# Rearranging the last steps before the scans of a state-space layer: B by TensorE, a square root by ScalarE, another order of loads and matmuls

## The chip, the cores and the metric

The kernel runs on one core of a Trainium2 chip. A core has five engines with their own instruction streams: TensorE (PE) for matmuls and transposes, VectorE (DVE), ScalarE (ACT), GpSimd (POOL), and SyncE (SP), which here only issues DMAs. They meet through semaphores. SBUF is the working memory of 128 partitions, PSUM the memory that matmuls write, DRAM the large memory outside, reached by DMA. The metric is device time in microseconds (us); several runs are made and their median is compared.

## The reference

Four layers follow one another, each normalised, applied and added to the residual x of 2 x 512 tokens by 512: a Mamba layer, a feed-forward layer with 4-bit weights, an attention over heads within each token, and a latent mixture layer. The change lies in the first layer; it also touches when the 4-bit weights of the second are unpacked. Cut to that:

```python
proj = hidden_states @ W_in.T                  # 512 -> 2 x 1024
x, gate = proj[..., :D_IN], proj[..., D_IN:]
x = silu(causal depthwise convolution of x with K = 4 taps, plus conv_b)
ssm = x @ W_x.T                                # 1024 -> 32 + 16 + 16
ts, Bm, Cm = ssm[..., :R], ssm[..., R:R + N], ssm[..., R + N:]
ts, Bm, Cm = rms_forward(ts), rms_forward(Bm), rms_forward(Cm)
dt = softplus(ts @ W_dt.T + b_dt)
A = -exp(A_log)
def step(state, inp):                          # state: 1024 channels x 16
    dt_t, B_t, C_t, u_t = inp
    state = state * exp(dt_t[..., None] * A) + (dt_t * u_t)[..., None] * B_t[:, None, :]
    return state, einsum('bdn,bn->bd', state, C_t)
y = (scan of step over 512 tokens + x * D) * silu(gate)
out = y @ W_out.T
```

`rms_forward` divides by the root of the mean square plus 1e-6, for ts, B and C apart. The weights of the second layer are `q * s - (z + 1) * s` with 4-bit q, eight to a 32-bit word.

## The kernel before

Channels lie on partitions, in 8 chunks of 128, and the 512 tokens of a batch in the free dimension. The two batches are b = 0 and 1. Code up to line 643 is the head; lines 650 to 1115 are the scan stage.

**The head** normalises x of batch 0 and transposes it (lines 570 to 585), then loops over the chunks c (line 593): TensorE projects a chunk into PSUM (`px`, line 597), ScalarE evicts it with one tap and the bias (`evict_x`, 468), VectorE adds three taps (`conv`, 475), ScalarE applies Silu (609), and TensorE multiplies the chunk by W_x into the 64 rows of ts, B and C for each token (`ranks_of`, 489). TensorE is two chunks ahead of the ranks.

**Words.** Beside that loop the 4-bit weights are unpacked. A "word" here is one of the eight 4-bit places of the packed gate and up weights for one cut of 512 columns; the head does two cuts, so 16 words (`GateUpWords`, lines 235 to 307). For each, VectorE extracts the nibble (233) and subtracts the zero points (293), GpSimd multiplies by the scales (295) and issues a DMA of 256 KB to DRAM (300). Three words are begun before the first convolution and finished after it; each later chunk has one or two (lines 605 to 616), and three stand around the norm of the ranks (618 to 634). A word's result lies in one of four rotating buffers, which is free once its DMA has landed.

**The last chain.** When the last chunk's ranks are there, the gate of chunk 0 is projected (626, four float32 matmuls, which the trace shows as eight passes). `ranks_norm` (494) squares on ScalarE, reduces on VectorE, raises to the power -0.5 on GpSimd (508) and multiplies on VectorE. TensorE transposes the result (524) to rows (`pt`). `ranks_out` (527) copies B and C rows to SBUF (`bc`), sends them to DRAM (`scr`, 531) and copies ts to `dtT`. `states` (535) then reads each group of two B or C rows back from `scr`, broadcast to 128 partitions: 16 loads of 512 KB on SP's queue, B0, C0, B1, C1 and so on. Behind them on SP's queue stand the four tiles of x of batch 1 (`load_x`, 641), then weights. dt of chunk 0 is a matmul (548) and a Softplus (553).

**The scan stage.** For each batch and chunk there are 8 scans s of two states each. ScalarE makes exp(dt A) into one of two PSUM tiles `da` (1002); VectorE multiplies `du` = dt u by B into `bx` (`times_B`, 1018) and scans (`scan`, 1022); GpSimd multiplies by C (`times_C`, 1028); TensorE sums over states with an identity matrix (1050). `du` lies in PSUM. The order on each engine is the order of the loop at line 1072, which `pin` (401) fixes; other work (gates, the projection of batch 1, its norm `norm_job`, the last eight words) is run in turns by `tick` (671). In that order `bn_stats` on the first tile of batch 1's x stands on VectorE between scans 4 and 5, and `times_B(2)` in front of scan 1. At most 8 DMAs of SP's queue are under way: an issue waits until the eighth before it has landed.

Of the kernel before, what the change touches and what calls it, by code (L numbers as in the profile page):

```python
# [9 lines left out]
F32 = mybir.dt.float32  # L10
F16 = mybir.dt.float16
I32 = mybir.dt.int32
AF = mybir.ActivationFunctionType
# [43 lines left out]
def tile_sandwich(  # L57
# [177 lines left out]
    class GateUpWords:  # L235
# [9 lines left out]
            word_loads(self.parts(zds), n0, n1, qw, z, s, 2, eng, engz)  # L245
            return [(n0, n1, qw, z, s, q, w, j) for j in range(PACK)]

        def start(self, dq, zds):
            def tl(dt, tag, bufs):
                return lambda name: dq.tile([P, CW], dt, tag=tag, name=f"{tag}_{name}", bufs=bufs)  # L250

            self.todo = []
            for a in range(2):
                nm = f"gu{a}"
                self.todo += self.cut(
                    a,
                    (tl(I32, "qw", 2)(nm), tl(F16, "z", 2)(nm), tl(F16, "s", 2)(nm),
                     tl(I32, "q", 3), tl(F32, "w", 4)),
                    zds, nc.gpsimd, nc.sync,
                )  # L260

# [9 lines left out]
                zds, nc.sync, nc.sync,  # L271
            )

        def steps(self):
            n0, n1, qw, z, s, q_, w_, j = self.todo.pop(0)
            n, nm = n1 - n0, f"gu{n0}_{j}"
            q = q_(nm)
            beside = bool(scans)

            while beside and (now[0] % 2 == 0 or pool_at[0] == (now[0] - 1) // 2 - 1):  # L280
                yield 1
            nibble(q[:, :n], qw[:, :n], j)
            yield 2
            w = w_(nm)
            if beside:
                nc.scalar.copy(w[:, :n], q[:, :n])
                yield 2
                yield from pool_turn()
                nc.gpsimd.tensor_sub(w[:, :n], w[:, :n], z[:, :n])
                yield 1  # L290
                yield from pool_turn()
            else:
                nc.vector.tensor_sub(w[:, :n], q[:, :n], z[:, :n])
                yield 2
            nc.gpsimd.tensor_mul(w[:, :n], w[:, :n], s[:, :n])
# [9 lines left out]
        def word(self):  # L305
            for _ in self.steps():
                pass

    def once(dq):
# [112 lines left out]
    with ExitStack() as mamba:  # L422
# [30 lines left out]
            dtT.append(t_)  # L453
        wx = smp.tile([P, NCH, N_ROW], F32, name="wx")
        nc.gpsimd.dma_start(out=wx, in_=W_x)
        Bbs = [[None] * NGI for _ in range(B)]
        Cbs = [[None] * NGI for _ in range(B)]
        st = {}
# [35 lines left out]
        def ranks_norm(b, ps):  # L494

            sq = jrow(f"sq{b}")[:, : TB * N_ROW].rearrange("p (i r n) -> p i r n", i=TB, n=N_ST)
            nc.scalar.activation(sq.rearrange("p i r n -> p i (r n)"), ps, AF.Square)
            yield 2
            ss = stat.tile([P, TB, 3], F32, tag="ss", name=f"ss{b}")
            nc.vector.tensor_reduce(  # L500
                ss[:, :, 0], sq[:, :, : R_DT // N_ST].rearrange("p i r n -> p i (r n)"), AX.X, ALU.add
            )
            nc.vector.tensor_reduce(ss[:, :, 1:], sq[:, :, R_DT // N_ST :], AX.X, ALU.add)
            r = stat.tile([P, TB, 3], F32, tag="rr", name=f"rr{b}")
            nc.vector.tensor_scalar(r[:, :, 0], ss[:, :, 0], 1.0 / R_DT, 1e-6, ALU.mult, ALU.add)
            nc.vector.tensor_scalar(r[:, :, 1:], ss[:, :, 1:], 1.0 / N_ST, 1e-6, ALU.mult, ALU.add)
            yield 1
            nc.gpsimd.tensor_tensor(r, r, mhalf3, ALU.pow)
# [16 lines left out]
            return pt  # L525

        def ranks_out(b, pt):
            bc = jrow(f"bc{b}")
            nc.vector.tensor_copy(bc[R_B:N_ROW], pt[R_B:N_ROW])
            sc = dram.tile([N_ROW - R_B, S], F32, tag=f"scr{b}", name=f"scr{b}")  # L530
            nc.sync.dma_start(out=sc, in_=bc[R_B:N_ROW])
            scr.append(sc)
            nc.scalar.copy(dtT[b][:R_DT, :], pt[:R_DT])

        def states(b, gi):

            for lst, lo, nm in ((Bbs[b], 0, "B"), (Cbs[b], R_C - R_B, "C")):
                t_ = bcp.tile([P, NG, S], F32, tag=f"{nm}{gi}", name=f"{nm}{b}_{gi}")
# [7 lines left out]
        def dt_in(b, c):  # L546
            ps = mbank(f"pv{b}_{c}")
            nc.tensor.matmul(ps, wdt[:, ts(c, P)], dtT[b], start=True, stop=True)
            return ps

# [8 lines left out]
        with ExitStack() as p1:  # L559
# [28 lines left out]
            gw.start(dq, zds)  # L588
            nc.vector.tensor_scalar(A, A, -1.0, None, ALU.mult)
            diag(0)  # L590

# [1 line left out]
            for c in range(NCH):  # L593
                w = w_in(0, 0, c)
                ps = bank1(c, f"px0_{c}")
                for k in range(KH):
                    nc.tensor.matmul(
                        ps, w[:, k, ts(c % 2, P)], xT[0][:, k, :], start=(k == 0), stop=(k == KH - 1)
                    )
                    if k == 1 and c >= 2:  # L600
                        for i in range(TB):
                            ranks_of(0, c - 2, i, pr)
                uc = u[0][c] = new_u(f"u0_{c}")
                evict_x(c, ps, uc)
                early = [gw.steps() for _ in range(3 if c == 0 else 0)]
                for word in early:
                    next(word)
                conv(c, ps, uc)
                nc.scalar.activation(uc, uc, AF.Silu)
                for word in early:  # L610
                    for _ in word:
                        pass
                if c:
                    gw.word()
                if c in (2, 4, 6):
                    gw.word()

            late = gw.steps()
            for _ in range(2):
                next(late)  # L620
            for c in (NCH - 2, NCH - 1):
                for i in range(TB):
                    ranks_of(0, c, i, pr)
            pg = mbank("pg0_0")
            for k in range(KH):
                nc.tensor.matmul(
                    pg, w_in(1, 0, 0)[:, k, 0:P], xT[0][:, k, :], start=(k == 0), stop=(k == KH - 1)
                )
# [12 lines left out]
            with tc.issue_after(last.ins):  # L641
                load_x(1)
            pin()
# [6 lines left out]
        with ExitStack() as p2:  # L650
# [7 lines left out]
            das = []  # L658
            for i, ps_da in enumerate((ps_da0, ps_da1)):
                da = ps_da.tile([P, NG, S], F32, tag=f"da{i}", name=f"da{i}")  # L660
                nc.vector.memset(da[:, :, 0:1], 0.0)
                das.append(da)


            jobs = []
# [38 lines left out]
            MM = 0.86  # L704
            STEP = 3.5

            def in_proj(b, ps, w, e):
                for k in range(KH):
# [10 lines left out]
            def gate(b, c):  # L719
                w = w_in(1, b, c)  # L720
                if c + 2 - c % 2 < NCH:
                    w_in(1, b, c + 2 - c % 2)
                ps = yield from bank(f"pg{b}_{c}")
                yield from in_proj(b, ps, w, c % 2)
                spawn(gate_job(b, c, ps), 2)

            def x_job(c, ps):
# [709 lines left out]
```

## Time and profile before

| what | us |
|---|---|
| runs: median (lowest to highest) | 954.11 (953.85 to 956.48) |
| the profiled execution, its own time | 955.89 |
| its span, first to last instruction | 954.1 |
| VectorE busy from 24 to 50 us, in the convolution loop | 24.53 of 26.00 |
| TensorE's granted clock, 50 to 56 and 56 to 64 us | 0.71, 0.58 |
| TensorE idle in front of the last ranks, waiting for Silu | 4.1 |
| VectorE, start of the first and the last convolution | 20.00, 52.88 |
| VectorE, start of scans 0, 1 and 2 | 73.97, 80.03, 83.34 |
| VectorE idle in front of `times_B(0)` and `times_B(2)`, for B | 3.74, 1.32 |
| VectorE busy from 110 to 200 us, in the scan stage | 89.38 of 90.00 |

A row of the timeline gives the start, the length, the engine, the line, the instruction with what it writes and reads, how many, and in brackets how long the engine was idle before it and what ended that. "PEld" is the load of a matmul's weights, "SPq" an issue on SP's queue. Rows of one kind that follow each other are merged.

### The profile page before, as it was taken

To read this page: it belongs to the slowest core of one execution; us is meant where nothing else is said; L and a number is where in the kernel's file an instruction comes from. 1 tells how busy PE (TensorE), PEld (TensorE's weight loads), DVE (VectorE), ACT (ScalarE), POOL (GpSimd) and SP (SyncE) were. 2 spreads that over 40 slices of the span, in tenths; PEclk is the share of its full clock that TensorE was granted. 3 is DMA by queue.
4 is the path that set the end of the run, shared out by engine and by line. 5 is a ranking of instruction groups with operands and counts; after the bars stand their busy time and mean duration, and the time that the engine had idled before them with its cause. 6 is when DMAs were issued, how large, how long until landed. Compare 5 with 4: busy or idle time off the path is not lost.

```text
span 954.1 us, 7148 instructions
## 1 busy us (share of the span) xinstructions
PE 862.3 (90%) x2184; PEld 386.6 (41%) x2184; DVE 675.2 (71%) x783; ACT 420.2 (44%) x631; POOL 484.0 (51%) x351
## 2 busy tenths in 40 slices
PE   6977989779989899579999999998999998999994
PEld 3532434333534434234433444444544444445441
DVE  4968999999999998999999995535610034534225
ACT  3335775656666655476655640125320014322122
POOL 5665796777877777876877884440000000011002
PEclk9978999898999989889999999999999999998997
DMA  6439211010002854300111103455223221200101
GB/s 182 163 124 387 69 37 38 30 37 31 22 23 83 297 187 152 89 0 0 45 44 45 30 9 124 150 159 198 58 64 89 58 89 45 66 12 30 48 0 44
DMA packets 43816, 80.08 MB, mean 84 GB/s; under 512 B 7774, under 2 KB 20937, under 8 KB 43778
## 3 DMA queue, kind: packets, MB, share of 16 engines
q1 hardware_dynamic: 41506, 73.64, 23.6%
q0 software_dynamic: 1984, 5.47, 1.6%
q10 hardware_dynamic: 288, 0.52, 0.2%
q8 instruction: 17, 0.28, 0.1%
q14 instruction: 21, 0.17, 0.1%
HBM read 68.37 MB, written 11.24 MB: 83 GB/s over the span
## 4 chain that ended last, share of the span: by engine, by line
PE 46%; DVE 28%; issue 11%; POOL 5%; DMA 2%; ACT 1%; SPq 0%; DVEq 0%; POOLq 0%; ACTq 0%
DVE bx L1022 11%; DVE bx L1018 8%; PE pd L1365 6%; PE py L1050 5%; PE pup L1302 5%; PE fo L1155 4%; PE fu L367 3%; PE fo L1218 3%; POOL bx L1028 3%; PE fg L367 3%; PE fu L947 3%; PE fg L947 3%; PE po L1133 3%; PE po L916 2%; DVE u L475 2%
## 5 line engine op out<-in xcount | busy, mean ns | idle before, releaser
L1028 POOL TENSOR_TENSOR bx<-bx,C 128x1024 f32<-128x1024 f32 x128 | 302.0, 2360 | 115.3 <-DVE bx L1022 90.7
L1022 DVE TENSOR_TENSOR_SCAN bx<-da,bx 128x1024 f32<-128x1024 f32 x128 | 291.6, 2279 | 0.1
L1050 PE MATMUL py<-bx,ident 128*128 128x512 f32 x480 | 238.1, 626 | 35.6 <-POOL bx L1028 32.3
L1002 ACT ACTIVATE da<-dt,A 128x511 f32<-128x511 f32 x256 | 176.3, 691 | 161.6 <-DVE bx L1022 155.7
L1018 DVE TENSOR_TENSOR bx<-du,B 128x1024 f32<-128x1024 f32 x128 | 154.4, 1206 | 9.0 <-DMA B<-scr 5.1
L1050 PEld LDWEIGHTS py<-bx,ident 128*128 128x128 f32 x480 | 91.5, 198 | 164.1 <-issue 93.1
L1231 DVE TENSOR_TENSOR it<-it,fu 128x512 f32<-128x512 f32 (+1 forms) x11 | 7.6, 688 | 72.3 <-PE fu L367 72.3
L1302 PE MATMUL pup<-hT_l,wup 128*128 128x512 f32 x128 | 57.5, 604 | 0.0
L381 POOL TENSOR_TENSOR sd<-ve,half 128x4 f16<-128x4 f16 x2 | 2.1, 1045 | 109.0 <-DVE ve L379 109.0
L709 PE MATMUL pg<-xT,w_g 128*128 128x512 f32 x120 | 57.1, 604 | 0.0
L1365 PE MATMUL pd<-wdn,hid 128*128 128x512 f32 x128 | 55.3, 592 | 0.0
L127 POOL TENSOR_TENSOR rs_lo<-ve_lo,mhalf 128x1 f32<-128x1 f32 x8 | 5.5, 684 | 78.0 <-DVE ve_lo L125 78.0
L947 PE MATMUL fg<-hT_f,wg 128*128 128x512 f32 (+1 forms) x88 | 42.1, 597 | 0.0
L475 DVE SCALAR_TENSOR_TENSOR u<-px,ch,u 128x511 f32<-128x511 f32 (+2 forms) x48 | 35.8, 746 | 7.0 <-ACT u L468 5.9
L367 PE MATMUL fg<-hT_f,wg 128*128 128x512 f32 (+1 forms) x88 | 40.2, 593 | 0.7 <-ACT hT_f L171 0.7
L947 PE MATMUL fu<-hT_f,wu 128*128 128x512 f32 (+1 forms) x88 | 40.7, 592 | 0.0
L367 PE MATMUL fu<-hT_f,wu 128*128 128x512 f32 (+1 forms) x88 | 39.8, 593 | 0.0
L1218 PE MATMUL fo<-wd,it 128*128 128x512 f32 (+1 forms) x88 | 39.6, 592 | 0.0
L1155 PE MATMUL fo<-wd,it 128*128 128x512 f32 (+1 forms) x88 | 38.0, 593 | 1.6 <-DMA wd<-wd_d 1.6
L1365 PEld LDWEIGHTS pd<-wdn,hid 128*128 128x128 f32 x128 | 24.2, 190 | 30.7 <-issue 30.1
L1302 PEld LDWEIGHTS pup<-hT_l,wup 128*128 128x128 f32 x128 | 24.5, 195 | 28.8 <-issue 28.8
L1230 ACT ACTIVATE it<-fg 128x512 f32<-128x512 f32 (+1 forms) x11 | 6.6, 597 | 65.7 <-PE fg L367 65.7
(224 smaller groups left out, 1161.4 us busy)
## 6 DMA issues: line engine op xcount, KB each, us to landing
wo<-in_W_outT SPq DMA_DIRECT2D x20, 512.0 KB
B<-scr SPq DMA_DIRECT2D x16, 512.0 KB
C<-scr SPq DMA_DIRECT2D x16, 512.0 KB
wg<-wgu_d SPq DMA_DIRECT2D x10, 512.0 KB
wu<-wgu_d SPq DMA_DIRECT2D x10, 512.0 KB
w_x<-in_W_in SPq DMA_DIRECT2D x8, 512.0 KB
wgu_d<-w_gu POOLq DMA_DIRECT2D x16, 256.0 KB, 2.3
w_g<-in_W_in SPq DMA_DIRECT2D x8, 512.0 KB
```

Of the source, the lines that this page charges most:

```text
L367: nc.tensor.matmul(ps[:m], w[:, kc, e * P : e * P + m], hT[:, kc, :], start=(kc == 0), stop=(kc == KH - 1),)
L709: nc.tensor.matmul(ps, w[:, k, ts(e, P)], xT[b][:, k, :], start=(k == 0), stop=(k == KH - 1))
L947: nc.tensor.matmul(ps[:m], wt[j][a][:, kc, e * P : e * P + m], hT[:, kc, :], start=(kc == 0), stop=(kc == KH - 1),)
L1002: nc.scalar.activation(das[s % 2][:, i, 1:], st["dt", b, c][:, 1:], AF.Exp, scale=A[:, c, n : n + 1])
L1018: nc.vector.tensor_mul(bx, st["du"].unsqueeze(1).to_broadcast([P, NG, S]), Bbs[b][gi])
L1022: nc.vector.tensor_tensor_scan(flat, das[s % 2].rearrange("p n t -> p (n t)"), flat, 0.0, ALU.mult, ALU.add)
L1028: nc.gpsimd.tensor_mul(bxs[s], bxs[s], Cbs[b][s % NGI])
L1050: nc.tensor.matmul(st["y"], ident, bx[:, i, :], start=False, stop=last)
L1155: nc.tensor.matmul(fo[t], its[i][:m, ts(t, P)], w[:m, e], start=(i == 0), stop=(i == len(IC) - 1),)
L1218: nc.tensor.matmul(fo[t], its[i][:m, ts(t, P)], w[:m], start=(i == 0), stop=(i == len(IC) - 1),)
L1302: nc.tensor.matmul(ps, w[:, kc, ts(e, P)], src[kc], start=(kc == 0), stop=(kc == KH - 1))
L1365: nc.tensor.matmul(pd, hid[kc][:, ts(i, P)], wdn[kc], start=(kc == 0), stop=(kc == INT // P - 1),)
```

## The change

- The norm of batch 0's ranks takes a square root on ScalarE and a reciprocal on VectorE in place of the power on GpSimd. A root of one column stands on ScalarE between the gate's Silu and the norm; the function table for the root is loaded there.
- B's first group comes to the first product from TensorE, which multiplies the rows `bc` by `pick`, a matrix of copied identity columns that GpSimd makes at the start, into the second `da` tile. The first product reads dt u from SBUF (`d0`) and B from there; the copy of dt u to PSUM comes after it.
- Loads from `scr` go in the order B1, C0, B2, C1, ..., B7, C6, C7, B0. x stays behind them.
- The gate of chunk 0 is projected in front of the last chunk's ranks; half of the gate of chunk 1 stands in front of the transposes, its other half in the scan stage. `pt` and the first dt use other PSUM banks. ts is copied out of `pt` before B and C.
- Of the 16 words, four are begun before the first convolution, and two of these subtracted before it. Words 6, 7, 10 and 13 (counted from 0) are converted by ScalarE and subtracted by GpSimd. The last word stands behind the copy of B and C. Nibbles have four buffers, and the last four words' results lie in buffers of the gates.

As the program is built, VectorE's statistics of x still stand between scans 4 and 5, and `times_B(2)` in front of scan 1; VectorE's copy of B and C waits for ScalarE's copy of ts, since both read the same tile. On ScalarE a word's conversion stands between Silu of a chunk and the next chunk's eviction.

```diff
@@ words
-        def start(self, dq, zds):
+        def start(self, dq, zds, apart):
...
-                     tl(I32, "q", 3), tl(F32, "w", 4)),
+                     tl(I32, "q", 4), lambda n: apart(n) or tl(F32, "w", 4)(n)),
...
-        def steps(self):
+        def steps(self, eng=nc.vector):
...
             w = w_(nm)
-            if beside:
+            if eng is nc.vector:
+                eng.tensor_sub(w[:, :n], q[:, :n], z[:, :n])
+                yield 2
+            else:
                 nc.scalar.copy(w[:, :n], q[:, :n])
                 yield 2
-                yield from pool_turn()
-                nc.gpsimd.tensor_sub(w[:, :n], w[:, :n], z[:, :n])
+                if beside:
+                    yield from pool_turn()
+                eng.tensor_sub(w[:, :n], w[:, :n], z[:, :n])
...
@@ head
+        pick = trow("pick")[:, : NG * P].rearrange("p (n q) -> p n q", n=NG)
+        for n in range(NG):
+            nc.gpsimd.tensor_copy(pick[:, n, :], ident[:, R_B + n : R_B + n + 1].to_broadcast([P, P]))
...
-            nc.gpsimd.tensor_tensor(r, r, mhalf3, ALU.pow)
+            if b:
+                nc.gpsimd.tensor_tensor(r, r, mhalf3, ALU.pow)
+            else:
+                nc.scalar.activation(r, r, AF.Sqrt)
+                nc.vector.reciprocal(r, r)
...
         def ranks_out(b, pt):
-            bc = jrow(f"bc{b}")
+            bc = st["bc"] = jrow(f"bc{b}")
+            nc.scalar.copy(dtT[b][:R_DT, :], pt[:R_DT])
             nc.vector.tensor_copy(bc[R_B:N_ROW], pt[R_B:N_ROW])
...
-            nc.scalar.copy(dtT[b][:R_DT, :], pt[:R_DT])
...
-                early = [gw.steps() for _ in range(3 if c == 0 else 0)]
+                early = [gw.steps() for _ in range(4 if c == 0 else 0)]
                 for word in early:
                     next(word)
+                for word in early[:2]:
+                    next(word)
                 conv(c, ps, uc)
...
-                if c in (2, 4, 6):
-                    gw.word()
-            late = gw.steps()
-            for _ in range(2):
-                next(late)
-            for c in (NCH - 2, NCH - 1):
-                for i in range(TB):
-                    ranks_of(0, c, i, pr)
+                for _ in range((0, 0, 2, 0, 1, 0, 1, 0)[c]):
+                    gw.word(nc.gpsimd)
+            for i in range(TB):
+                ranks_of(0, NCH - 2, i, pr)
             pg = mbank("pg0_0")
...
-            for n, _ in enumerate(ranks_norm(0, pr)):
-                if n == 2:
-                    for _ in late:
-                        pass
-                    gw.word()
-                    gw.word()
+            for i in range(TB):
+                ranks_of(0, NCH - 1, i, pr)
             g[0][0] = new_g0("g0_0")
             nc.scalar.activation(g[0][0], pg, AF.Silu)
-            ranks_out(0, ranks_rows(0, mbank("pt0")))
+            root = stat.tile([P, 1], F32, tag="root", name="root", bufs=1)
+            nc.scalar.activation(root, half[:, 0:1], AF.Sqrt)
+            half_gate = mbank("pg0_1")
+            for k in range(KH // 2):
+                nc.tensor.matmul(
+                    half_gate, w_in(1, 0, 0)[:, k, P : 2 * P], xT[0][:, k, :], start=(k == 0), stop=False
+                )
+            for _ in ranks_norm(0, pr):
+                pass
+            ranks_out(0, ranks_rows(0, bank1(0, "pt0")))
             for gi in range(NGI):
-                last = states(0, gi)
-            dt_out(0, 0, dt_in(0, 0))
+                if gi + 1 < NGI:
+                    states(0, gi + 1, "B")
+                states(0, gi, "C")
+            last = states(0, 0, "B")
+            gw.word()
+            dt_out(0, 0, dt_in(0, 0, bank1(0, "pv0_0")))
@@ scan stage
+            B0 = das[1]
+            for n in range(NG):
+                nc.tensor.matmul(
+                    B0[:, n, :], pick[R_B : R_B + N_ST, n, :], st["bc"][R_B : R_B + N_ST],
+                    start=True, stop=True,
+                )
+            nc.vector.memset(das[0][:, :, 0:1], 0.0)
...
-            new_du(0)
+            d0 = jrow("d0")
+            nc.vector.tensor_mul(d0, u[0][0], st["dt", 0, 0])
+            st["du"] = ps_du.tile([P, S], F32, tag="du", name="du0_0")
             exps(0)
+            bxs[0] = bxp.tile([P, NG, S], F32, tag="bx", name="bx0_0_0")
+            nc.vector.tensor_mul(bxs[0], d0.unsqueeze(1).to_broadcast([P, NG, S]), B0)
+            nc.scalar.copy(st["du"], d0)
+            nc.vector.memset(das[1][:, :, 0:1], 0.0)
             exps(1)
-            times_B(0)
```

More of the change, by code (lines that the diff above doesn't have):

```diff
@@ L278, in steps @@
             beside = bool(scans)
+            if beside:
+                eng = nc.gpsimd
             while beside and (now[0] % 2 == 0 or pool_at[0] == (now[0] - 1) // 2 - 1):
@@ L284, in steps @@
             w = w_(nm)
-            if beside:
+            if eng is nc.vector:
+                eng.tensor_sub(w[:, :n], q[:, :n], z[:, :n])
+                yield 2
+            else:
                 nc.scalar.copy(w[:, :n], q[:, :n])
                 yield 2
-                yield from pool_turn()
-                nc.gpsimd.tensor_sub(w[:, :n], w[:, :n], z[:, :n])
+                if beside:
+                    yield from pool_turn()
+                eng.tensor_sub(w[:, :n], w[:, :n], z[:, :n])
                 yield 1
[L291 to L294, printed above, removed]
+                if beside:
+                    yield from pool_turn()
             nc.gpsimd.tensor_mul(w[:, :n], w[:, :n], s[:, :n])
@@ L303, in steps, with word @@
             yield 2
-        def word(self):
-            for _ in self.steps():
+        def word(self, eng=nc.vector):
+            for _ in self.steps(eng):
                 pass
@@ L532, in ranks_out, with states @@
             scr.append(sc)
-            nc.scalar.copy(dtT[b][:R_DT, :], pt[:R_DT])
-        def states(b, gi):
+        def states(b, gi, which="BC"):
             for lst, lo, nm in ((Bbs[b], 0, "B"), (Cbs[b], R_C - R_B, "C")):
+                if nm not in which:
+                    continue
                 t_ = bcp.tile([P, NG, S], F32, tag=f"{nm}{gi}", name=f"{nm}{b}_{gi}")
@@ L544, in states, with dt_in @@
             return ins
-        def dt_in(b, c):
-            ps = mbank(f"pv{b}_{c}")
+        def dt_in(b, c, ps=None):
+            ps = ps or mbank(f"pv{b}_{c}")
             nc.tensor.matmul(ps, wdt[:, ts(c, P)], dtT[b], start=True, stop=True)
@@ L587, in tile_sandwich @@
             zds = zeros(dz, [gate_z, up_z], KH, INTER, "gu")
-            gw.start(dq, zds)
+            apart = [f"gu{CUTS[1][0] * PW}_{j}" for j in range(PACK - 4, PACK)]
+            gw.start(dq, zds, lambda n: new_g0(f"w_{n}") if n in apart else None)
             nc.vector.tensor_scalar(A, A, -1.0, None, ALU.mult)
@@ L660, in tile_sandwich @@
                 da = ps_da.tile([P, NG, S], F32, tag=f"da{i}", name=f"da{i}")
-                nc.vector.memset(da[:, :, 0:1], 0.0)
                 das.append(da)
+            B0 = das[1]
[5 more added lines that the diff above has]
+            nc.vector.memset(das[0][:, :, 0:1], 0.0)
             jobs = []
@@ L705, in tile_sandwich, with in_proj @@
             STEP = 3.5
-            def in_proj(b, ps, w, e):
-                for k in range(KH):
+            def in_proj(b, ps, w, e, k0=0):
+                for k in range(k0, KH):
                     nc.tensor.matmul(
@@ L722, in gate @@
                     w_in(1, b, c + 2 - c % 2)
-                ps = yield from bank(f"pg{b}_{c}")
-                yield from in_proj(b, ps, w, c % 2)
+                if (b, c) == (0, 1):
+                    turns.append([f"pg{b}_{c}", None])
+                    ps = half_gate
+                    yield from in_proj(b, ps, w, c % 2, KH // 2)
+                else:
+                    ps = yield from bank(f"pg{b}_{c}")
+                    yield from in_proj(b, ps, w, c % 2)
                 spawn(gate_job(b, c, ps), 2)
```

## The prediction

> **What bounds the kernel now.** I read the chain of waits first, then the timeline from the convolution loop to the sixth scan, then the DMA share by window. The chain of waits, up to 100 us (start, length, what):
>
> ```profile
> 51.48 1.47 DVE w_gu L293
> ...
> 57.93 5.95 PE pg L626 x8
> ...
> 65.07 2.49 DMA scr<-bc
> ...
> 69.52 9.34 DMA B<-scr
> ...
> 93.36 0.61 DVE st_n L761
> ```
>
> Up to 56 us VectorE's convolutions and its work on the 4-bit words set the pace. Then eight gate passes of 0.74 us hold the transposes, the round trip of B and C through DRAM follows, and from 80 us VectorE is dense: nearly all that follows to 330 us is its products and scans. A shift of the scans' start should therefore reach the end, unless a later VectorE instruction waits for something that did not shift. The timeline (start, length, engine, line, instruction) shows the three places that decide:
>
> ```profile
> 27.26 1.76 DVE L233 TENSOR_SCALAR q_gu<-qw_gu 128x512 int32<-128x512 int32 x1
> ...
> 27.55 1.17 POOL L295 TENSOR_TENSOR w_gu<-w_gu,s_gu 128x512 f32<-128x512 f32 x1
> ...
> 33.17 1.27 POOL L295 TENSOR_TENSOR w_gu<-w_gu,s_gu 128x512 f32<-128x512 f32 x1 [1.31 <-DVE w_gu L293]
> ...
> 33.52 1.47 DVE L293 TENSOR_TENSOR w_gu<-q_gu,z_gu 128x512 f32<-128x512 int32 x1
> ...
> 59.16 2.40 POOL L508 TENSOR_TENSOR rr<-rr,mhalf 128x12 f32<-128x12 f32 x1 [0.56 <-DVE rr L506]
> ...
> 83.88 4.01 SPq L83 DMA_DIRECT2D x<-in_x_in  x4
> ...
> 93.28 0.68 DVE L761 BATCH_NORM_STATS2 st_n<-x 128x6 f32<-128x512 f32 x1
> ...
> 95.27 0.34 SPq L111 DMA_DIRECT2D w_x<-in_W_in  x1
> ```
>
> First: a nibble or subtraction of VectorE that meets a GpSimd multiply lasts until that ends (1.76 for 0.42, 1.47 for 0.69). Second: the power on GpSimd takes 2.40 us. Third: the statistics of batch 1's x stand between scans 4 and 5 on VectorE. The last row waited 0.33 us for the fourth x, so the four x (256 KB, 0.62 us apart at the stream's rate) land near 93.2, 93.9, 94.5 and 95.2. The first is just in time for 93.28. By windows the 16 DMA engines are full from 76 to 91 us (share 1.02 and 1.03, 420 GB/s): B, C and x are one stream, each half megabyte 1.24 us behind the last (issues at 76.33, 77.58, 78.88 wait each for a landing).
>
> **The change, part by part.** Times count from E, the end of the last convolution (55.19 before).
>
> *The loop.* A step from one convolution to the next took 3.73 us with one word, 5.25 with two. Now three steps carry GpSimd words: VectorE saves the subtraction, but ScalarE converts the nibble (0.47 for 352 columns at L286, 0.57 for a 512 copy at L1010; I take 0.6) ahead of the next eviction, and GpSimd subtracts too (0.85 for 352 columns at L289, so 1.2 for 512).
> - Convolution 1 to 2: two subtractions now run before convolution 0, in VectorE's idle 5.1 us, so GpSimd starts its queue some 5 us sooner and the nibble of 27.26 finds it free: 4.64 becomes 3.8, -0.85.
> - 2 to 3: 2.31 of convolution, 0.42 + 0.69 + 0.5 for a word and a nibble, the next nibble held 1.2 by the multiply, 0.6 + 0.7 for conversion and eviction: 6.4 for 5.25, +1.15, with three words instead of two.
> - 3 to 4: GpSimd has 2 x 3.3 us of words 6 and 7 (1.2 + 1.17 + 0.9 of DMA issue); a hold of 0 to 0.65, +0.1 taken.
> - 4 to 5: a nibble held 1.1 by word 8's multiply, then subtraction, nibble, conversion: 6.2 for 5.25, +0.95.
> - 5 to 6: a nibble held: +0.25. 6 to 7: 0.
>
> Sum +1.6. Bounds: with no hold at all, -0.4 (0.85 gained, 0.4 for the third word in the second step); with a hold of 0.36 us on average (60% of GpSimd's time in such work, 0.6 us left of one) for each of the 14 nibbles and subtractions behind convolution 2, +5.0 - 0.85 = +4.2. I take the sum, the hits being placed one by one.
>
> [...]
>
> *Square root on ScalarE.* Silu (0.63), the gate's Silu (0.54 apart, 0.60 long), a table load of 1.28 and a 128x1 root (0.2) end at E+2.7; the Square ends at E+3.1, as before (58.35, E+3.16). The last ranks are ready at E+1.9, since the gate's eight passes (0.43 each, as at 50 us) now fill TensorE's 4.1 us of idle in front of them: the table load takes that gain. Reductions and scaling: 0.72, E+3.85. Root 0.2 and reciprocal 0.23 (178 ns for 128x4 at L383, 550 for 128x64 at L1268) with two hand-overs, E+4.45, then 0.5 of products: E+4.97 against E+6.89.
>
> [...] Here the load at 65.67 lasts 1.28 and the next ACTIVATE starts at 66.96, 0.01 behind it. [...]
>
> *Transposes.* The half gate's four passes end at E+3.7, before the rows are ready. Transposes E+5.05 to E+5.65, against E+9.13. The copy of dt's rows now goes first (0.57), and B and C (0.68) wait for it: E+7.05, and scr is sent at E+7.08 against E+9.88: -2.8. If TensorE's clock is halved (passes of 0.86, as after the 4.1 us idle), the half gate ends at E+6.3 and 1.3 to 1.8 of it is lost.
>
> *B by TensorE.* B0 needs two matmuls of 16 rows, four passes, at most 2.2 us; dt is ready at E+8.2, d0 at E+8.9 to E+10.1 (word 15's multiply may hold it), the product at E+11 at most, the exponentials (1.28 + 1.41) at E+10.9, scan 0 ends near E+13.4, 70.2 us against 76.26. Only scan 1 waits for that, and it waits for B2 longer: cover of over 4 us. The two copies that make `pick` cost nothing: 4.44 + 2 x 0.40 (a 128x128 product on GpSimd) ends before 5.29, when the first power comes; at worst 0.1.
>
> *Order of B and C.* B2, for which scan 1 waits (78.86), goes from fifth to third in SP's queue: 2 x 1.24 = 2.5 us sooner. C0 stays second (75.1 before, by the issue that waited for it) and comes with the shift of scr alone, 73.9, behind scan 0 and well ahead of scan 1's turn at GpSimd. B0 goes last, and is needed only for chunk 1. Scan 1 then starts 1.2 + 2.5 = 3.7 sooner.
>
> *What is late next.* x still stands seventeenth. VectorE reaches its statistics at 93.28 - 3.7 = 89.6, and x lands at 93.2 - 1.2 = 92.0. It waits 2.4 us, and scan 5 with everything queued behind it (products, scans, so GpSimd's C products and TensorE's sums) moves by the shift of scr alone.
>
> **Sum:** +1.6 - 2.8 = -1.2 us; the order's 2.5 us are given back at x. Span 954.1 - 1.2 = 952.9. The profiled run took 955.89, 1.8 more than its span; the median of the runs, 954.11, is close to the span, so the shift is put on it: **952.9 us**.
>
> **The rivals.**
> 1. *The loop costs nothing* (-0.4): 2.8 + 0.4 = 3.2, 950.9. For it: VectorE has three fewer subtractions there. Against: each converted word sits on ScalarE between Silu and eviction, where the step's length is set.
> 2. *x does not bind*, the stream is faster or the statistics can wait: 3.7, 950.4. Against: full DMA engines and x arriving on time to 0.1 us.
> 3. *The port takes it all* (slower): holds of +4.2 in the loop, net +1.4: 955.5. Place: nibbles at L233 beside GpSimd's subtract and multiply pairs. It decides from a loop loss of 2.8 us. For it: 2.23 us for one 352-column nibble at 142.32. Against: between these pairs GpSimd issues its DMA for 0.9 us.
> 4. *The transposes still wait* (TensorE at half clock): -1.2 + 1.8 = +0.6, 954.7. Against: idles of 0.86 and 1.96 us left passes at 0.43; the longest idle now would be 1.8.
>
> **How the numbers follow.** Forecast 0.50 (own range 951.5 to 954.2), rivals 0.15, 0.10, 0.15, 0.10. The range 949.9 to 956.0 takes in the rivals' middles and a scatter like that of the three runs. A measurement of this kernel can tell 0.3%, 2.9 us, from no change: below 951.2 lie most of rivals 1 and 2 and a tail of the forecast, 0.24; above 957.0 only a tail of rival 3, 0.08; between them 0.68.
>
> **What would show it.** Right: the last convolution starts near 54.5 (52.88 before), scr is issued near 63.9, scan 1 starts near 76.3, and VectorE is idle some 2 us in front of the statistics of x near 89.6. Wrong: a last convolution at or before 52.5 (rival 1), no idle there (rival 2), scr later than 65.1 (3 if the loop is late, 4 if the half gate's passes take 0.86).

## The result, and the profile after

The changed kernel took 957.60 us in the median of 12 runs (953.07 to 958.88), the kernel before 955.49 us in 12 runs on the same chip: a ratio of the means of 1.0018, interval 1.0002 to 1.0034. So it is about 0.2% slower, less than the 0.3% that the prediction's classes call a difference, but in the other direction than forecast and outside the range of 949.9 to 956.0. The profiled execution of the changed kernel took 955.66 us with a span of 953.7, that of the kernel before 955.89 with 954.1.

The chain of waits of the changed kernel (start, length, what) shows other steps in the head:

```profile
57.63 1.28 ACT L648
...
63.29 1.61 DMA scr<-bc
...
69.56 12.32 DMA B<-scr
81.90 9.60 DMA x<-in_x_in
```

Neither GpSimd's power nor the eight gate passes are there. In their place stands the table load for the root. The round trip of B is still there (12.32 us for 9.34), and behind it comes x, which the chain of before did not hold. VectorE's timeline of the changed kernel, its idle time in brackets:

```profile
62.58 0.68 DVE L542 COPY bc<-pt 32x512 f32<-32x512 f32 x1 [1.33 <-ACT dtT L541]
...
73.60 1.22 DVE L1055 TENSOR_TENSOR bx<-du,B 128x1024 f32<-128x1024 f32 x1 [2.17 <-DMA B<-scr]
74.75 2.28 DVE L1059 TENSOR_TENSOR_SCAN bx<-da,bx 128x1024 f32<-128x1024 f32 x1
...
91.53 0.69 DVE L798 BATCH_NORM_STATS2 st_n<-x 128x6 f32<-128x512 f32 x1 [3.45 <-DMA x<-in_x_in]
...
92.35 2.25 DVE L1059 TENSOR_TENSOR_SCAN bx<-da,bx 128x1024 f32<-128x1024 f32 x1
...
111.18 0.66 DVE L1093 TENSOR_TENSOR g<-g,py 128x512 f32<-128x512 f32 x1
...
111.76 0.77 DVE L233 TENSOR_SCALAR q_gu<-qw_gu 128x352 int32<-128x352 int32 x1
...
119.09 0.70 DVE L233 TENSOR_SCALAR q_gu<-qw_gu 128x352 int32<-128x352 int32 x1
```

Scan 1 starts 5.28 us sooner than in the profile of before (74.75 against 80.03). In front of x's statistics 3.45 us of that are lost; scan 5 is 1.74 us ahead, the product of chunk 0 (line 1093) 1.92. Then two nibbles of 352 columns last 0.77 and 0.70 us, where the first two in the profile of before lasted 0.32 each, and the lead is 0.84. That much two profiles tell; but in them the changed kernel is still 0.57 us ahead at the last product of a chunk (578.37 against 578.94), and 0.4 us at the end. The 2 us that it lost in the runs were not to be seen, and this is what the experiments were for.

### The profile page after: what moved, and what is told of

Same layout as the page of the kernel before. It is cut to its first block, busy times and chain, and to the rows that moved or that the text cites. A ratio compares the mean times of both kernels' runs of the same rounds, so it can differ in the third digit from the quotient of the medians.

```text
span 953.7 us, 7163 instructions
## 1 busy us (share of the span) xinstructions
PE 860.8 (90%) x2188; PEld 385.4 (40%) x2188; DVE 672.4 (71%) x780; ACT 424.1 (44%) x638; POOL 486.8 (51%) x356
## 4 chain that ended last, share of the span: by engine, by line
PE 48%; DVE 24%; issue 9%; POOL 7%; DMA 3%; ACT 2%; SPq 0%; DVEq 0%; POOLq 0%; ACTq 0%
DVE bx L1059 10%; DVE bx L1055 6%; PE py L1087 6%; PE pd L1408 6%; POOL bx L1065 5%; PE pup L1345 5%; PE fo L1198 4%; PE fg L371 4%; PE fu L371 4%; PE fo L1261 3%; PE fu L984 3%; PE fg L984 3%; PE po L1176 3%; PE po L953 2%; DVE u L483 2%
## 5 line engine op out<-in xcount | busy, mean ns | idle before, releaser
L1087 PE MATMUL py<-bx,ident 128*128 128x512 f32 x480 | 234.9, 620 | 41.4 <-POOL bx L1065 36.3
```

What stands on the lines that cost most here:

```text
L1087: nc.tensor.matmul(st["y"], ident, bx[:, i, :], start=False, stop=last)
```

## The experiments

Twelve kernels were run, four at a time on one chip with the kernel before beside them: its median was 957.14 us (35 runs) beside the first four, 955.62 (31) beside the next, 955.97 (19) beside the last. Ratios are of the means, to these runs, so they can differ by 0.1% or so from the ratio of the medians.

### Both kernels again

Four further profiles of the unchanged kernels: the kernel before as `b_again`, `b_third` and `b_fourth`, the changed one as `a_again`.

> The kernel before, unchanged, for its clock and a second profile of it. Theory (the 0.2% are drawn by TensorE's clock: half-clock stretches of 3.41 us, worth 1.7 us each where the matmuls set the pace, fall differently in each execution): its runs spread over 953 to 959 us again, the slower ones at a lower mean clock, and its median lies within 0.7 us of the changed kernel's. Rival (something in the change costs 2 us in every execution): its median is 1.5 to 2.5 us below that of the changed kernel, at the same spread.

> The changed kernel, unchanged. Theory of the clock: ratio to the kernel before between 0.9993 and 1.0007, and in the second profile the scans' stage ends 0.3 to 1 us sooner than in that of the kernel before, as in the first. Rival (a steady cost): ratio 1.0015 to 1.0025 again, and the second profile shows where the head's 1.9 us turn into a loss.

`b_again`: 955.74 us, ratio 0.9991 (0.9974 to 1.0009); `a_again`: 956.94 us, 1.0009 (0.9993 to 1.0024). Neither theory was quite it. The first comparison's 0.18% has become 0.09%; a kernel differs from itself by as much. But in the spread lay something better, a second profile of the kernel before that was not like its first. It had scan 1 at 78.32 instead of 80.03, and lost 2.25 us near 149, where the first lost nothing. The matmuls of batch 1's first u in `b_again`:

```profile
142.25 8.06 PE L709 MATMUL px<-xT,w_x 128*128 128x512 f32 x12 [0.67 <-ACT xT L787]
```

and in the first profile of before:

```profile
143.74 5.42 PE L709 MATMUL px<-xT,w_x 128*128 128x512 f32 x12 [0.67 <-ACT xT L787]
```

The same twelve passes took 8.06 instead of 5.42 us, since the granted clock was halved for 10.24 us, from 137.4 to 147.6 (0.50 there, 1.00 behind it). VectorE's convolution then waited 2.17 us for ScalarE's eviction, and every later scan stood 2.25 us later. So the baseline itself draws lots, and the one profile of it that I had was one draw. Two more were taken at the end:

> The kernel before, unchanged: a third profile of it. Theory (its first profile, against which the changed kernel's head stood 5.3 us ahead, had drawn a late landing of B for scan 1, 1.7 us, and the second lost 2.2 us to a half-clock stretch on the matmuls of batch 1's first u near 149 us; without either the kernel before is about 1.2 us ahead of the changed one at scan 52): scan 1 starts 78.0 to 78.9, and where no half-clock stretch meets those matmuls, scan 52 stands at 286.0 to 287.0 (changed kernel 287.4 to 287.6). Rival (the late landing is the rule): scan 1 at 79.8 to 80.3, scan 52 at 288.

> The kernel before, unchanged: a fourth profile of it, with the same expectations as the third; the two are there to see which of the two draws is the common one.

The times of events in the six profiles (us; scans counted from 0):

| event | before, 1st | 2nd | 3rd | 4th | changed, 1st | 2nd |
|---|---|---|---|---|---|---|
| first convolution | 20.00 | 19.72 | 18.98 | 18.96 | 19.23 | 19.23 |
| last convolution | 52.88 | 52.58 | 51.85 | 51.82 | 54.10 | 54.10 |
| `scr` sent | 65.07 | 64.68 | 63.54 | 63.49 | 63.29 | 63.29 |
| first load of B sent | 67.62 | 66.94 | 65.96 | 65.88 | 64.96 | 64.97 |
| x sent | 83.88 | 82.16 | 81.18 | 81.83 | 81.90 | 81.67 |
| scan 1 | 80.03 | 78.32 | 77.64 | 79.26 | 74.75 | 74.84 |
| scan 5 | 94.09 | 92.38 | 91.70 | 93.33 | 92.35 | 92.10 |
| scan 9 | 110.91 | 109.20 | 108.52 | 110.15 | 108.98 | 108.73 |
| scan 12 | 121.69 | 119.98 | 119.31 | 120.93 | 120.85 | 120.58 |
| scan 52 | 288.06 | 288.59 | 285.68 | 287.29 | 287.61 | 287.38 |
| last product of a chunk | 578.94 | 578.71 | 576.63 | 577.25 | 578.37 | 577.55 |

The third goes the theory's way and beyond its numbers (77.64 for 78.0 to 78.9, and 285.68 for 286.0 to 287.0). The fourth, with scan 1 at 79.26 and scan 52 at 287.29, fits neither set. So that a late B is the exception is not shown: scan 1 comes anywhere from 77.6 to 80.0. Two things are drawn in the head of the kernel before: when the first convolution starts (1.04 us between profiles), and when VectorE's first product runs after `scr` is sent (7.6 to 10.0 us later, 10.0 in the fourth). The second is not B's doing, except in the first profile. In the other three the first product waits for the last word of the head, whose result is on its way to DRAM; in the fourth:

```profile
66.11 0.58 POOL L300 DMA_DIRECT2D wgu_d<-w_gu  x1 [0.30 <-POOL w_gu L295]
...
73.48 1.23 DVE L1018 TENSOR_TENSOR bx<-du,B 128x1024 f32<-128x1024 f32 x1 [6.15 <-DMA wgu_d<-w_gu]
```

This DMA took 2.6 us from issue to landing in the first profile, where it was issued 0.44 us ahead of the first load of B, and 5.3, 5.5 and 7.2 us in the others, where the two were issued together (0.07 us ahead to 0.23 behind). B itself was there 1.0 to 3.1 us before it was taken: the ninth load, which is issued once the first has landed, goes out at 71.40, 70.35 and 70.38. (In the first profile the tenth goes out at 75.13, the second having landed at 75.11.) The product's buffer belongs to a pool that is opened when that of the words is closed; that the two share memory is the likely reason, which was not shown. Nor does scan 1 wait for its B in these three profiles, only in the first (1.32 us). The changed kernel's first product waits for neither DMA: it takes TensorE's B at 66.77. Against the third, the lead at scan 1 is 2.89 us, not 5.28, and this is all lost when x is waited for: +0.65 us at scan 5, +1.54 at scan 12, +1.93 at scan 52. VectorE in the third profile of before:

```profile
77.64 2.28 DVE L1022 TENSOR_TENSOR_SCAN bx<-da,bx 128x1024 f32<-128x1024 f32 x1
...
90.89 0.68 DVE L761 BATCH_NORM_STATS2 st_n<-x 128x6 f32<-128x512 f32 x1
...
91.70 2.26 DVE L1022 TENSOR_TENSOR_SCAN bx<-da,bx 128x1024 f32<-128x1024 f32 x1
...
107.15 0.32 DVE L233 TENSOR_SCALAR q_gu<-qw_gu 128x352 int32<-128x352 int32 x1
```

No brackets: it does not wait for x, though it asks for it at 90.89, sooner than the changed kernel gets it. And its nibble lasts 0.32.

### x sent sooner

```diff
             for gi in range(NGI):
...
-                states(0, gi, "C")
+                last = states(0, gi, "C")
+                if gi == 4:
+                    with tc.issue_after(last.ins):
+                        load_x(1)
             last = states(0, 0, "B")
...
-            with tc.issue_after(last.ins):
-                load_x(1)
```

> The changed kernel with batch 1's four x tiles loaded ahead of the last six loads of B and C instead of behind them. Theory (x's place on the queue gives the head's gain back): x lands near 86.5 instead of 91.5, VectorE's 3.45 us of idle before x's statistics go, scan 5 starts near 89 (92.35 before the edit), and the product of chunk 0 stands near 108 (111.18). If a shift of the scans reaches the end, the time falls by 2.5 to 3.5 us against the changed kernel. Rival (a later wait takes it): scan 5 moves as said, but the time moves by less than 1 us. Second rival (B of chunk 7, now behind x, lands too late): the idle time moves to the product of scan 7, near 92, and scan 8 stands where it stood.

Measured: 954.24 us, 0.9984 (0.9967 to 1.0001), 2.7 us below `a_again` on the same chip. VectorE of `x_ahead`:

```profile
74.80 2.28 DVE L1060 TENSOR_TENSOR_SCAN bx<-da,bx 128x1024 f32<-128x1024 f32 x1
...
88.04 0.69 DVE L799 BATCH_NORM_STATS2 st_n<-x 128x6 f32<-128x512 f32 x1
...
88.87 2.26 DVE L1060 TENSOR_TENSOR_SCAN bx<-da,bx 128x1024 f32<-128x1024 f32 x1
```

The idle time is gone, scan 5 starts at 88.87 and the product of chunk 0 at 107.69, as expected. At scan 52 the lead over the changed kernel's first profile is 3.44 us, at the last product of a chunk 2.88, though this profile's loop started 0.56 us later. So the shift is carried through 490 us nearly whole, and x's place on the queue is what took the head's gain.

### The order of B and C alone

```diff
             for gi in range(NGI):
-                if gi + 1 < NGI:
-                    states(0, gi + 1, "B")
-                states(0, gi, "C")
-            last = states(0, 0, "B")
+                last = states(0, gi)
```

> The changed kernel with B and C sent in the order of the kernel before (B and C of each pair of states in turn, from the first), scan 0 still from TensorE's B. Theory (x binds behind scan 4, so the order alone is worth nothing there): scan 1 starts 2.5 to 3.9 us later than 74.75, the idle time before x's statistics shrinks by the same, scan 5 stays at 92.3 within 0.3, and the time within 0.5 us of the changed kernel's. Rival (the order is worth its 2.5 us): scan 5 and the end stand 2 to 4 us later.

Measured: 956.59 us, 1.0000 (0.9984 to 1.0015), 0.35 us from `a_again`. Scan 1 starts at 78.44, 3.7 us later, and the wait for x is 0.20 us instead of 3.45; scan 5 starts at 92.81, 0.46 later, a little more than the 0.3 allowed. The new order gains 3.7 us at scan 1, and as long as x stands behind all 16 loads, it is worth nothing at scan 5.

### TensorE's B

On top of `x_ahead`, scan 0's product takes B from DRAM, which is sent first:

```diff
+            states(0, 0, "B")
             for gi in range(NGI):
...
-            B0 = das[1]
...
+            new_du(0)
             exps(0)
...
-            nc.vector.tensor_mul(bxs[0], d0.unsqueeze(1).to_broadcast([P, NG, S]), B0)
...
             exps(1)
+            times_B(0)
```

> The changed kernel with x ahead, without TensorE's B: B of the first pair of states is sent first and scan 0 waits for it, the rest in order of need. Theory (VectorE does the first product, scan 0 and two more products before scan 1, so TensorE's B takes 1.15 + 2.2 + 1.15 us out of the path behind the first landing): scan 1 starts near 79.3 (74.80) and all scans behind it 4.5 us later, the time 3.5 to 4.5 us above x_ahead's. Rival (the order alone brings the gain, TensorE's B only one place in the queue): scan 1 near 76.1, the time 1 us above.

Measured: 958.55 us, 1.0036 (1.0018 to 1.0054). Scan 1 starts at 78.62, 3.8 us later than in `x_ahead`; 1.0 us more goes at scan 4, which waits for an exponential, and the last product of a chunk stands 4.02 later. TensorE's B takes a product, a scan and a second product out of the path behind the first landing. With x out of the way this is worth 4.9 us up to scan 68 and 4.0 at the last product; the medians differ by 4.3, on two chips.

### The words of the loop back on VectorE

On top of `x_ahead`, `gw.word(nc.gpsimd)` becomes `gw.word()`: ScalarE's conversion and GpSimd's subtraction of four words go back to one subtraction on VectorE.

> The changed kernel with x ahead, and the four words of the loop that subtract on GpSimd (with ScalarE's conversion) on VectorE instead, at the same places. Theory (holds by GpSimd's second pass cost more than the subtraction saves, as the prediction's +1.6 has it): the last convolution starts 0.3 to 1.2 us sooner than 54.1, and scan 1 by the same. Rival (VectorE's own 4 x 0.69 us weigh more): the last convolution starts 0.3 to 1.5 us later, and scan 1 by the same.

Measured: 953.03 us, 0.9975 (0.9957 to 0.9992). The absolute bounds were badly chosen, since the start of the loop is drawn: this profile's first convolution was at 20.08. From the first to the last convolution it takes 34.13 us, the changed kernel 34.87, the kernel before 32.88 (52.88 less 20.00). So conversion and GpSimd's subtraction together cost the loop 0.74 us; the other 1.25 us of its lengthening are left for the words moved into it, by subtraction, not by a run. Although its loop started 0.29 us later than that of `x_ahead`, this profile stands 0.44 us ahead of it at scan 1; 0.1 is left at the last product of a chunk.

### The nibbles of the scan stage

In the changed kernel the two long nibbles lie beside GpSimd's multiplies, here in its timeline of GpSimd:

```profile
109.98 4.77 POOL L1065 TENSOR_TENSOR bx<-bx,C 128x1024 f32<-128x1024 f32 x2
...
118.31 1.28 POOL L719 TENSOR_TENSOR g<-th,g 128x512 f32<-128x512 f32 x1
```

The first nibble is issued at 111.76 and is done at 112.53, 0.2 us behind the end of the first of the two products; the second, from 119.09, is done at 119.79, 0.2 behind the gate's product. On top of `x_ahead` the words begin two ticks sooner:

```diff
-            spawn(words_job(), 4)
+            spawn(words_job(), 2)
```

> The changed kernel with x ahead, and the words of the scans' stage begun two ticks sooner, which puts the first nibbles at other places between scans. Theory (0.8 us of the head's gain go where the nibbles at 108.27 and 115.6 meet a GpSimd product and last 0.77 and 0.70 instead of 0.32): the first two nibbles last 0.3 to 0.4, and scan 15 starts 0.6 to 0.9 us sooner against scan 9 than in x_ahead (22.88 us between them). Rival (the loss is not in the nibbles, or another product is met): 22.7 us or more between scans 9 and 15.

Measured: 953.88 us, 0.9982 (0.9962 to 1.0001). VectorE of `x_words_2`:

```profile
102.04 0.34 DVE L233 TENSOR_SCALAR q_gu<-qw_gu 128x352 int32<-128x352 int32 x1
...
112.84 0.34 DVE L233 TENSOR_SCALAR q_gu<-qw_gu 128x352 int32<-128x352 int32 x1
```

From scan 9 to scan 15 it takes 22.04 us instead of 22.88, what the kernel before takes (22.02 in its third profile): 0.84 us, as expected. But that stretch flatters the edit, since the first nibble now stands in front of scan 8, outside it. From scan 7 to scan 15 it is 28.98 us instead of 29.57: 0.59. Other nibbles moved too (the one of 2.2 us, near 138 in `x_ahead`, is now near 173.5), and from scan 15 to scan 52 another 0.63 us is gained. Against this, B of the seventh pair, sent behind x, came 0.5 us late; with 0.37 us at scan 1, scan 5 stands 0.98 later, so that scan 52 is only 0.24 us sooner. The last product of a chunk stands 1.10 sooner, but the other 0.9 come between scans 68 and 72, near 345 us, where profiles shift for another reason (next section).

### Which copy goes first

The changed kernel copies ts in front of B and C. Around batch 1's rows VectorE shows (the changed kernel):

```profile
286.89 0.68 DVE L542 COPY bc<-pt 32x512 f32<-32x512 f32 x1 [2.84 <-ACT dtT L541]
```

On top of `x_ahead` the old order:

```diff
-            nc.scalar.copy(dtT[b][:R_DT, :], pt[:R_DT])
             nc.vector.tensor_copy(bc[R_B:N_ROW], pt[R_B:N_ROW])
+            nc.scalar.copy(dtT[b][:R_DT, :], pt[:R_DT])
```

> The changed kernel with x ahead (as in x_ahead), and in both batches VectorE's copy of B's and C's rows in front of ScalarE's copy of dt's rows, as in the kernel before. Theory (the second of the two copies waits for the first, so the changed order makes the round trip of B and C later): scr is sent 0.6 us sooner than 63.85, scan 1 starts near 74.2 (74.80), and in front of batch 1's copy VectorE waits 2.2 us instead of 2.84, so that scan 52 stands 1.2 us sooner than in x_ahead and the sums' end near 579.4 (580.6). Rival (the copies only seem chained; each waits for the transposes): scan 1 and scan 52 within 0.2 us of x_ahead's.

VectorE of `x_bc_first`:

```profile
62.91 0.68 DVE L541 COPY bc<-pt 32x512 f32<-32x512 f32 x1 [0.72 <-PE pt L536]
...
282.83 0.68 DVE L541 COPY bc<-pt 32x512 f32<-32x512 f32 x1 [2.06 <-PE pt L536]
```

Measured: 952.83 us, 0.9962 (0.9944 to 0.9981). In both batches the copy now waits for TensorE, 0.6 to 0.8 us less. In batch 1 that is carried to scan 52 (283.54 against 284.17), but not the 1.2 us expected there: this profile's loop started 0.33 us later, and scan 1 stands where it stood (74.74). At the last product of a chunk nothing is left (575.64 against 575.49): it is 0.61 us sooner up to scan 68 and 0.50 later at scan 72. There, near 345 us, the scans are behind the loads of `wo` and TensorE's work on them (in the changed kernel TensorE waits 3.30 us for `wo` up to 337.54), and profiles shift against each other by about 1 us; which of the two does it was not tried. The time alone, 1.4 us below that of `x_ahead` on another chip, settles nothing.

### Both undone, and all together

`two_undone` is the changed kernel with the last two edits, x where the change has it. `best` has them and x ahead of the last four loads (`gi == 5`).

> The changed kernel (x where the change has it), with VectorE's copy of B's and C's rows first again and the words of the scans' stage two ticks sooner. Theory (these two cost the changed kernel 0.63 and 0.84 us behind x, which takes all that the head gains): scan 5 within 0.6 us of 92.35 (x decides), scan 9 to 15 takes 22.0 instead of 22.9 us, scan 52 stands 1.2 to 1.9 us sooner than 287.5, and the time 0.5 to 1.5 us below the changed kernel's 957.0, at the kernel before's within 0.1%. Rival (neither reaches the end): time within 0.4 us of the changed kernel's.

> The changed kernel with x ahead of the last four loads of B and C (one pair later than in x_ahead, since there B of the seventh pair came 0.5 us late once the words had moved), VectorE's copy first, and the words two ticks sooner. Theory: no idle time on VectorE between scan 1 and scan 9 but 0.2 us, scan 5 near 88.6, scan 15 near 127.2, scan 52 near 282.3 (287.6 in the changed kernel), and a time of 951.5 to 953.5 us, 3.5 to 5.5 us below the changed kernel's. Rival (x now lands too late for its statistics): 1 to 2 us idle before scan 5, time about 953.5 to 954.5.

| kernel | us | ratio (interval) | scan 1 | scan 5 | scan 52 | last product |
|---|---|---|---|---|---|---|
| changed, `a_again` | 956.94 | 1.0009 (0.9993 to 1.0024) | 74.84 | 92.10 | 287.38 | 577.55 |
| `two_undone` | 952.40 | 0.9962 (0.9945 to 0.9978) | 73.81 | 90.67 | 284.12 | 574.28 |
| `best` | 949.74 | 0.9939 (0.9918 to 0.9961) | 74.06 | 88.35 | 281.78 | 571.89 |

`two_undone` gained more than I had said: 4.5 us below `a_again` for 0.5 to 1.5 (both beside the kernel before on their own chip, 0.47%), and 3.3 to 3.5 us at scan 52 for 1.2 to 1.9. From scan 5 to scan 52 it takes 193.45 us, the changed kernel 195.26 and 195.28, the kernel before 193.96 to 193.98 where no clock stretch fell. I had left out that x follows `scr`: with the copy first `scr` is sent at 62.53 instead of 63.29, and x comes with it (its statistics at 89.84 instead of 91.53; of these 1.7 us 0.8 are `scr`, the rest is a quicker stream: the fourth load lands 11.3 us after `scr` is sent instead of 12.2, why is not known). Scan 9 to 15 takes 22.03 us, as expected. And 0.23 us more is gained outside the span (1.78 us for 2.01). `best` came below the 951.5 to 953.5 us expected of it, and beats both kernels, by 6.2 us the one before (medians); VectorE waits for nothing between scan 1 and scan 9 but 0.2 us, and from the second of these kernels to the third scan 5 gains 2.32 us, the last product 2.39 and the time 2.66.

## Why the prediction was wrong

*The loop, +1.6:* measured +1.99 (34.87 for 32.88), the mechanism as said: nibbles held by GpSimd, and evictions behind conversions. By steps it was less exact than in sum: 1 to 2 took 3.73 (3.8 said), 2 to 3 6.48 (6.4), 3 to 4 5.46 (3.83), 4 to 5 5.23 (6.2), 5 to 6 3.88 (3.97). The hits on a nibble and a subtraction came one step sooner than placed (1.74 at 36.69, 1.47 at 38.53).

*The last chain, -2.8:* right. `scr` was sent 6.88 us behind the last convolution's end (7.08 said), with the root, the reciprocal and the transposes where they were expected; against the third and fourth profile of before, whose transposes came sooner, it is -2.5. Rival 4 did not come.

*B by TensorE, costing nothing:* right; what I gave no price for is that it was needed, 4 us as soon as x no longer decides. Nor did I see that it takes the landing of a word's result out of the path, which held the first product in three of four profiles of before.

*The order of B and C, given back at x:* right in kind. Its 2.5 us came from the wait for B in front of scan 1, which the other three profiles of before do not have; in the changed kernel it was worth 3.7 at scan 1. x was waited for 3.45 and 3.10 us (2.4 said), and landed at 91.5 (92.0 said). `old_order` and `x_ahead` show it from both sides. Rival 2 fell.

*"Scan 5 with everything queued behind it ... moves by the shift of scr alone":* this step failed. It puts the way behind scan 5 at the same length in both kernels; from scan 5 to scan 52 the changed one takes 1.3 us more (195.26 and 195.28 for 193.96 to 193.98). Two things in the change cost it, and neither is in the sum. The new turns on VectorE and GpSimd put the first two nibbles of the scan stage beside GpSimd multiplies: from scan 5 to scan 15 39.50 and 39.49 us for 38.82 to 38.83, 0.67 more, of which 0.59 came back when they were moved. And the order of the copies, which I priced in the head, where it is hidden in the chain's gain, acts a second time on batch 1's rows: between scans 51 and 52 6.95 and 6.75 us for 6.32 to 6.34, and 6.16 with the old order. With both undone the 1.3 us are gone (`two_undone`, 193.45). The prediction itself listed the copy's wait and the holds by GpSimd, and the trace showed the scan stage to be all VectorE; what was not done was to follow each changed helper to its second call, and to read the new places of the old instructions in the scan stage. Rival 3, holds by GpSimd, had the right mechanism in the wrong place, the loop; that a port is behind them, as its name says, no run shows.

*The base, 954.11:* also at fault. It is the median of three runs. Over all 111 runs of the kernel before that stand beside these kernels the median is 955.82 us and the spread (standard deviation) 2.1; the range took the three for the scatter.

*The sum, made again.* Mean of the profiles, scan 5: 92.88 before, 92.23 changed: -0.65 (-1.2 said; of the -1.74 in the first pair, 0.77 was the later start of the loop in the profile of before). At scan 52, without the 2.25 us of clock in the second profile, 286.84 and 287.50: +0.65 (+0.1 with them left in). Outside the span the changed kernel takes 2.01 us (24 runs, 1.96 to 2.08), the one before 1.78 (12 runs, 1.73 to 1.83): +0.23. Together +0.9 us, or 0.09%. The runs say +0.09% and +0.18% with intervals that hold both. Behind the last product of a chunk, where the code is the same, the changed kernel took 375.3 and 377.1 us, the one before 375.0 to 375.2 in four profiles; two profiles are too few to add this as a cost or to call it a draw. How much of the first 2.1 us was a lucky draw for the kernel before stays open, and it can't be told from profiles that each show one execution.

## What to carry to other kernels

A shift is worth what the first instruction behind it that waits for something unshifted leaves of it: look along the engine's own order for the last load of the queue, and move that with the shift. An edit in a helper is to be priced at each call, and a rearranged order by the new neighbours of the instructions that nobody meant to move. Where a gain of 1 us is at stake in 950, one profile of the base is a draw; four showed scan 1 spread over 2.4 us, and the wait that decides it was another one in three of them than in the first.

## What the runs showed of the hardware

- Every half-clock stretch in the 14 profiles that lies whole within the span and behind the first full-clock one lasts a multiple of 3.41 us (3.41, 6.83, 10.24, 13.65). Where the stretches fall differs from execution to execution: from 137.9 us on the clock was halved for 3.41 us in the first profile of the kernel before, from 137.4 on for 10.24 in the second. The price is seen once: from scan 15 to scan 51 the kernel before took 151.07 us in the profile where such a stretch met twelve passes that VectorE was waiting for, and 148.80 to 148.83 in the three others, with half-clock stretches at other places. The code behind the last product of a chunk is the same in all these kernels, and took 375.0 to 375.6 us in ten profiles, 377.1 to 379.1 in four; the two longest of these have three stretches between 650 and 700 us, the others at most two; that these are the cause was not shown.
- The table load at 57.63 lasts 1.28 us, and ScalarE's next activation starts at 58.92, 0.01 behind it, as the row of before had it.
- The long nibbles beside a GpSimd multiply end 0.2 us behind it in the scan stage, 0.3 in the loop (36.69 plus 1.74, behind 36.97 plus 1.17). Not every nibble that meets one is long: in the changed kernel the one at 52.32 took its usual 0.42 us, though a multiply ran from 52.49 for 1.27. Nor did the power on GpSimd hold VectorE: while it ran from 59.16 for 2.40 us in the kernel before, VectorE's subtraction at 59.49 and nibble at 60.10 took their usual 0.69 and 0.42 us. What holds the long ones was not shown.
- Two copies from one PSUM tile, one by ScalarE from rows 0 to 31 and one by VectorE from rows 32 to 63, never overlap in these traces: whichever is second in the program starts when the first ends (62.58 behind 61.97 plus 0.57). Whether the chip or the program's semaphores ask for it was not tried.
- The time outside the span varies by 0.13 us at most between the runs of one kernel (1.73 to 1.85 in the kernel before, 1.96 to 2.08 in the changed one), and differs between kernels (means of 1.78 to 2.11 us). Why was not found.
